# Adjacency tiles as one contiguous piece of a DRAM row, and features read in natural order, in a four-layer graph network

## The chip, the cores and the metric

The kernel runs on one core of a Trainium2 chip. The metric is device time in microseconds (us) of one execution, lower is better. One execution of each kernel is also recorded by the hardware profiler: its span starts with the first instruction and ends with the last. In all that follows the engines are TensorE (PE in the profile, with PEld for its weight loads), VectorE (DVE), ScalarE (ACT), GpSimd (POOL) and SyncE (SP), which here only issues transfers.

## What is computed

There are N = 3327 nodes with D = 64 features and one dense 3327 x 3327 matrix `adj` (with few entries that are not zero). Four layers each normalise the features, apply relu, run a graph network, and add the result to x:

```python
def layer(x, gnn):
    h = jnp.maximum(layernorm(x), 0.0)
    return x + gnn(h, adj)

# gnn 0: two gated cells
m = adj @ (h @ W);  gi = m @ wih.T + bih;  gh = h @ whh.T + bhh
r, z = sigmoid(i_r + h_r), sigmoid(i_z + h_z);  n = tanh(i_n + r * h_n)
h = relu((1 - z) * n + z * h)
# gnn 1: weights by rank of a nonzero in its row, at most the last 100 count
rank = jnp.cumsum(adj != 0, axis=1)
w = mask * jnp.where(pos > 0, 0.5 ** (k - pos), 0.0)
out = w @ (h @ weight) + bias
# gnn 2: three hops with w = adj * adj
x = (w @ x) @ W.T + b
# gnn 3: two hops
x = jnp.tanh(jnp.concatenate([adj @ x, x], axis=1) @ W[k])
```

So the adjacency (or its mask, or its square) is multiplied eight times with 64 features a node: kinds PLAIN, PLAIN, RANKED, SQUARED, SQUARED, SQUARED, PLAIN, PLAIN. In gnn 1 the order of the columns of `adj` matters, since ranks are counted along them; everywhere else a renumbering of the nodes cancels out.

## The kernel before

**Layout.** The 3327 nodes are padded to 3328 = 26 blocks of 128. A node stands at (s, b, p): half s of two, block b of 13 in it, partition p. All work on node features is done for both halves at once: half 0 and half 1 of a chunk share an instruction, the TensorE products for them go to the upper and lower 64 columns of the array side by side. Blocks b are cut into four chunks, `CH[0..3]` = blocks 0-2, 3-5, 6-8, 9-12, so that chunks 0 to 2 have 384 columns per half and chunk 3 has 512. Chunks 0 and 1 form group 0, chunks 2 and 3 group 1. For the last product, chunk 1 is cut in two parts (blocks 3-4 and block 5, `PARTS`).

**Tiles.** The transposed adjacency lies in DRAM as 3328 rows (sources) of 3328 columns (targets). A `Tile(q, g)` is the 128 rows of source block q, and of the columns those of group g, for both halves: two runs of 768 (group 0) or 896 (group 1) fp32 values out of each row, 3,072 or 3,584 bytes each. `load` issues it as one DMA on SP's queue (L411) into one of 20 buffers (`slots`, "adj" in the profile). Each tile serves one or two of the eight products. 234 tiles are loaded in all, 26 for each of nine passes: `alone(0, 0)` is product 0 for group 0, `joint(1, 0)` products 0 and 1 for group 1, `joint(0, 1)` products 1 and 2 for group 0, and so on; `alone(0, 7)` is the last.

**Order.** The order of all instructions is the order in which the program writes them: `run()` walks a list of units (product, chunk, tile) and between them lets small tasks (layernorm, gates, transposes) advance by a budget of estimated microseconds (`spend`). Loads are written ahead while buffers are free. Products are issued at L613. The counts for gnn 1 are made during the first passes: VectorE turns a tile into a 0/1 mask (L472) and TensorE adds the masks up (L548). In product 2, masks are turned into ranks by a product with a triangle (L313 with `tri`), and ScalarE (L529) or VectorE (L527) turn ranks into powers of two. `square` (L446, L448) squares a tile on ScalarE or on VectorE, by the remainder of `q + c` modulo 3.

**Start.** Three DMAs bring the features `xs`: chunk 0 on SP, chunk 1 and then chunks 2 and 3 together on ScalarE's queue (L119), followed there by the weights of the first cell (L153, L156). SP goes on with the tiles. `warm_up` (L176) runs 28 TensorE instructions on the first features. `before_0(c)` computes the layernorm of a chunk on VectorE (L843 to L858), with the power -1/2 on GpSimd (L854). The first product L613 needs this for chunk 0.

**End.** `after_7(c)` evacuates the last product, applies the last dense product (L780) and tanh (L1041), adds to `xs` on VectorE (L1044), and writes the chunk to DRAM by one DMA (L1047): chunks of group 0 on SP, those of group 1 on ScalarE's queue.

**DRAM arrays.** The host lays the features out as [128, 13, 2, 64] (partition, block, half, feature) and takes the output in the same layout, with half s of block b being natural block 13 s + b. The rows and columns of the adjacency are in natural order.

Of the kernel before, what the change touches and what calls it, by code (L numbers as in the profile page):

```python
# [13 lines left out]
ALU = mybir.AluOpType  # L14
# [30 lines left out]
N, D = 3327, 64  # L45
# [38 lines left out]
def chunk_of(b):  # L84
    return next(c for c, (b0, b1) in enumerate(CH[:NC]) if b0 <= b < b1)


def sources_of(*chunks):
    return [s * NB + b for c in chunks for s in range(2) for b in range(*CH[c])]


def upper(n):
    return slice(n * D, (n + 1) * D)
# [3 lines left out]
def kernel(  # L97
# [17 lines left out]


    xs = const.tile([P, NB, 2, D], F32, name="xs")
    for queue, (g0, g1) in ((nc.sync, CH[0]), (nc.scalar, CH[1]), (nc.scalar, (CH[2][0], NB))):
        queue.dma_start(out=xs[:, g0:g1], in_=x[:, g0:g1])  # L119
    slots = [const.tile([P, 2, GWM], F32, name=f"adj{i}") for i in range(NBUF)]  # L120
    mhalf = const.tile([P, 8], F32, name="mhalf")
    nc.gpsimd.memset(mhalf, -0.5)
    bd = const.tile([P, 4, P], F32, name="bd")
# [47 lines left out]
    def warm_up():  # L171

        i, ps = take()
        for n in range(7):
            for h in range(2):
                nc.tensor.matmul(ps[upper(h), :3 * D], xs[:, 0, h, :], xs[:, 0:3, 0], start=True, stop=True)  # L176
        give(i)

    def fold_cell(cell):
# [166 lines left out]
    def groups(t):  # L346
        return t.rearrange("p b s d -> p (b s) d")
# [47 lines left out]
    class Tile:  # L395
# [12 lines left out]
        def load(self):  # L408
            self.slot = dead.popleft()
            w0 = self.b0 * P  # L410
            nc.sync.dma_start(out=slots[self.slot][:, :, :self.w],  # L411
                              in_=adjT[self.q * P:(self.q + 1) * P, :].rearrange(
                                  "p (s w) -> p s w", s=2)[:, :, w0:w0 + self.w])

        def view(self, *c):
            return slots[self.slot][:, :, self.cols(*c) if c else slice(0, self.w)]

        def used(self):
            self.uses -= 1
# [70 lines left out]
    def expand(k, c, t):  # L490

        if k == COUNT:
            return None
        w = width(c)
        if t is SPECIAL:
            g = c // 2
            w0 = (CH[c][0] - CH[GROUPS[g][0]][0]) * P
            finish(NC + 1 + g)
            return lastw[g][:, w0:w0 + w].bitcast(BF16)
        if KIND[k] == PLAIN or (KIND[k] == SQUARED and t.in_place):  # L500
            return t.view(c)
        if KIND[k] == SQUARED:
            room = Mask(t.w)
            wide = room.view.rearrange("p s w -> p (s w)").bitcast(F32)[:, :2 * w].rearrange("p (s w) -> p s w", s=2)
            square(wide, t.view(c), t.q + c)
            squared[k, c, t] = room
            return wide
        wide = work.tile([P, 2, CWM], I16, name="e", bufs=4)[:, :, :w]

        mask_pieces(t=t)
        for s in range(2):
            i, ps = take()
            mm(ps[:, :w], tri, t.mask.view[:, s, t.cols(c)])
            own = chunk_of(t.q % NB) in GROUPS[t.g]
            busy = any((k - 1, ch) in sums for ch in GROUPS[t.g])
            if t.g == 1 and not own and not relief["squares"]:

                on_vector = s and c == GROUPS[1][1]
            elif relief["pieces"]:
                on_vector = s and (t.q + c) % 4
            else:
                on_vector = s and (own if t.g == 0 and (own or busy) else c == GROUPS[t.g][1] or t.g == 1 and not own)
            if on_vector:
                nc.vector.tensor_scalar(wide[:, s], ps[:, :w], BITS, 0.0, op0=ALU.add, op1=ALU.max)  # L527
            else:
# [35 lines left out]
    def last_sources(g):  # L564

        w = sum(width(c) for c in GROUPS[g])
        w0 = CH[GROUPS[g][0]][0] * P
        room = Mask(w)
        v = room.view.rearrange("p s w -> p (s w)").bitcast(F32)
        nc.gpsimd.memset(v, 0.0)  # L570
        yield 4.0
        rows = adjT.rearrange("(q p) (s n) -> q p s n", p=P, s=2)
        for s in range(2):
            nc.sync.dma_start(out=v[s * D:s * D + NQ], in_=rows[:, P - 1, s, w0:w0 + w])
        yield 12.0
        nc.vector.tensor_scalar(v, v, 0.0, 129.0 * TWO7, op0=ALU.not_equal, op1=ALU.mult)
        for c in GROUPS[g]:
            finish(("count", c))
        yield 1.0
        nc.vector.scalar_tensor_tensor(v, totals[g], -TWO7, v, op0=ALU.mult, op1=ALU.add)  # L580
        yield 1.5
        nc.scalar.activation(lastw[g], v, AF.Relu, bias=bitsb)
        room.free()

    def propagate(k, c, t, rhs, first, last):
        if k == COUNT:
            count(t, first, last)
            return
        w = width(c)
        if first:  # L590
            sums[k, c] = [take(sums=True) for _ in range(2 if k == 7 and c == PARTS[1] else 1)]
            sums[k, c] = [sums[k, c][0], sums[k, c][-1]]
        acc = sums[k, c]
        if t is SPECIAL:
            for ch in range(NC):
                while y[k][ch] is None:
                    advance(ch)
            terms = [[lasty[:, h, i, :] for h in range(2)] for i in range(3)]
            rhs = [rhs, rhs]
        else:  # L600
            s, b = divmod(t.q, NB)
            cs = chunk_of(b)
            if y[k][cs] is None:
                finish(cs)
            terms = [[yk[:, b - CH[cs][0], s, :]] * 2 for yk in (y[k][cs] if KIND[k] == RANKED else [y[k][cs]])]
            rhs = [rhs[:, h, :] for h in range(2)]
            if KIND[k] != RANKED:
                t.used()
            if (k, c, t) in squared:
                squared.pop((k, c, t)).free()  # L610
        for n, yq in enumerate(terms):
            for h in range(2):
                nc.tensor.matmul(acc[h][1][h * D:(h + 1) * D, :w], yq[h], rhs[h], start=first and n == 0,  # L613
                                 stop=last and n == len(terms) - 1)
# [102 lines left out]
    def run():  # L717
# [5 lines left out]
        for i, (k, c, t) in enumerate(units):  # L723
# [19 lines left out]
            relief["pieces"] = False  # L743
            if k != 2:
                mask_pieces(1 + len(pieces) // 6)
            elif not (c in GROUPS[0] and (t is SPECIAL or chunk_of(t.q % NB) in GROUPS[0])):
# [88 lines left out]
        for i in {acc[0][0], acc[1][0]}:  # L835
            give(i)

    def layernorm_relu(h, c, scale=None, pace=1.0, squares_on_scalar=False):
        n = 2 * blocks(c)
        v = groups(xchunk(c))  # L840
        st = work.tile([P, 4, 8], F32, name="st", bufs=4)
        xc = work.tile([P, 8, D], F32, name="t2")
        nc.vector.tensor_reduce(st[:, 0, :n], v, AX.X, ALU.add)  # L843
        nc.vector.tensor_scalar(st[:, 1, :n], st[:, 0, :n], 1.0 / D, None, op0=ALU.mult)
        nc.vector.tensor_tensor(xc[:, :n], v, st[:, 1, :n, None].to_broadcast([P, n, D]), ALU.subtract)  # L845
# [87 lines left out]
    def in_three(h, c):  # L933
# [11 lines left out]
        b0, b1 = CH[c]  # L945
        for s in range(2):
            for k in range(2):
                q = k * D + s * NB
# [87 lines left out]
    def after_7(c, acc):  # L1036
# [5 lines left out]
        give(v[0])  # L1042
        yield 0.8
        nc.vector.tensor_tensor(flat(xchunk(c)), flat(xchunk(c)), flat(t), ALU.add)  # L1044
        g0, g1 = CH[c]
        queue = nc.scalar if c in GROUPS[1] else nc.sync
        queue.dma_start(out=out[:, g0:g1], in_=xs[:, g0:g1])  # L1047

    after[:] = [after_0, after_1, after_2, after_3, after_4, after_5, after_6, after_7]

# [66 lines left out]
```

## Time and profile before

| | |
|---|---|
| time, median of 3 runs | 697.6 us (697.42 to 697.65) |
| profiled execution: its own time | 697.73 us |
| profiled execution: span | 695.7 us |
| TensorE granted clock, mean | 0.999 |
| tiles of 768 KB / 896 KB | 130 / 104 |
| read from HBM | 199.45 MB, 288 GB/s over the span |
| DMA packets | 68,693 (7,244 of them under 512 B) |

The page gives each engine's busy time and its share of the span, followed by its number of instructions. Lists of waits give "engine, tile, line <- what it waited for: us in total, times, longest". A line of the timeline has the start in us, the busy time in us, the engine (a "q" behind the name is its queue of issued transfers), the line of the program, the operation, the tiles, and in brackets the idle time of the engine just before, with what ended it.

### The profile page before, as it was taken

To read this page: it belongs to the slowest core of one execution; us is meant where nothing else is said; L and a number is where in the kernel's file an instruction comes from. 1 tells how busy PE (TensorE), PEld (TensorE's weight loads), DVE (VectorE), ACT (ScalarE), POOL (GpSimd) and SP (SyncE) were. 2 spreads that over 40 slices of the span, in tenths; PEclk is the share of its full clock that TensorE was granted. 3 is DMA by queue.
4 is the path that set the end of the run, shared out by engine and by line. 5 is a ranking of instruction groups with operands and counts; after the bars stand their busy time and mean duration, and the time that the engine had idled before them with its cause. 6 is when DMAs were issued, how large, how long until landed. Compare 5 with 4: busy or idle time off the path is not lost.

```text
span 695.7 us, 12589 instructions
## 1 busy us (share of the span) xinstructions
PE 681.0 (98%) x5072; PEld 380.4 (55%) x5072; DVE 355.3 (51%) x772; ACT 274.3 (39%) x426; POOL 77.8 (11%) x114
## 2 busy tenths in 40 slices
PE   7899999999999999999999999999999999999997
PEld 4686667645566785556444444343344444344587
DVE  5946745755997899757341106325271565005101
ACT  1013000403147878888998107722176500000101
POOL 5300000002480414111100000000000000000000
PEclk9999999999999999999999999999999999999999
DMA  9999998099879921792899569954997399917991
GB/s 341 401 400 406 403 407 274 1 349 389 277 242 376 317 96 60 259 316 80 311 361 351 206 216 409 404 227 131 396 370 264 110 399 405 405 75 268 404 403 65
DMA packets 68693, 201.31 MB, mean 289 GB/s; under 512 B 7244, under 2 KB 8372, under 8 KB 68636
## 3 DMA queue, kind: packets, MB, share of 16 engines
q1 hardware_dynamic: 65724, 199.08, 76.9%
q10 hardware_dynamic: 736, 1.23, 0.5%
q8 instruction: 40, 0.66, 0.4%
q0 software_dynamic: 2176, 0.20, 0.2%
q14 instruction: 17, 0.14, 0.0%
HBM read 199.45 MB, written 0.85 MB: 288 GB/s over the span
## 4 chain that ended last, share of the span: by engine, by line
PE 58%; DVE 1%; ACT 0%; POOL 0%; issue 0%; DVEq 0%; ACTq 0%; POOLq 0%
PE sum L613 54%; PE temp L313 3%; PE temp L780 1%; ACT e L529 0%; POOL st L854 0%; DVE both L834 0%; DVE e L527 0%; PE sum L313 0%; ACT both L830 0%; DVE y L858 0%; DVE y L850 0%; DVE t L845 0%; DVE st L851 0%; DVE st L843 0%; DVE xs L865 0%
## 5 line engine op out<-in xcount | busy, mean ns | idle before, releaser
L613 PE MATMUL sum<-adj,y 128*64 128x384 f32 (+3 forms) x3016 | 535.4, 501 | 1.5 <-DVE y L858 0.7
L613 PEld LDWEIGHTS sum<-adj,y 128*64 128x64 f32 x3016 | 248.8, 137 | 230.5 <-issue 196.9
L446 ACT ACTIVATE adj<-adj 128x768 f32<-128x768 f32 (+1 forms) x176 | 144.4, 892 | 45.9 <-PE sum L613 23.0
L472 DVE TENSOR_SCALAR adj<-adj 128x768 bf16<-128x768 f32 (+3 forms) x208 | 114.0, 597 | 32.6 <-PE temp L548 24.7
L613 PE MATMUL sum<-e,both 128*64 128x384 bf16 (+1 forms) x624 | 74.0, 339 | 0.5 <-DVE e L527 0.5
L529 ACT ACTIVATE e<-temp,bitsb 128x384 int16<-128x384 f32 (+1 forms) x120 | 67.8, 607 | 14.9 <-PE temp L313 9.1
L830 ACT COPY both<-sum 64x384 f32<-64x384 f32 (+3 forms) x17 | 8.1, 478 | 148.2 <-PE sum L613 148.2
L834 DVE COPY both<-sum 64x384 f32<-64x384 f32 (+3 forms) x13 | 7.3, 561 | 99.5 <-ACT both L830 98.9
L448 DVE TENSOR_TENSOR adj<-adj 128x768 f32<-128x768 f32 (+1 forms) x32 | 30.6, 1004 | 51.9 <-DMA adj<-in_adjT 33.1
L854 POOL TENSOR_TENSOR st<-st,mhalf 128x6 f32<-128x6 f32 (+1 forms) x16 | 24.9, 1553 | 287.8 <-DVE st L852 287.8
L313 PE MATMUL temp<-adj,tri 128*64 128x384 bf16 (+1 forms) x332 | 51.7, 341 | 1.3 <-ACT e L529 0.8
L613 PEld LDWEIGHTS <-both 128*64 128x64 bf16 x624 | 41.9, 110 | 18.3 <-issue 6.5
L477 POOL DMA_DIRECT2D adj<-totals x52 | 33.6, 648 | 52.6 <-PE temp L313 41.7
L313 PEld LDWEIGHTS <-tri 128*64 128x64 bf16 x416 | 29.2, 110 | 17.3 <-issue 9.8
L527 DVE TENSOR_SCALAR e<-temp 128x384 int16<-128x384 f32 (+1 forms) x46 | 28.3, 615 | 20.0 <-PE temp L313 9.6
L809 DVE STREAM_TRANSPOSE both<-y 32x96 f32<-32x96 f32 (+1 forms) x128 | 35.6, 278 | 2.9
L548 PE MATMUL temp<-adj,behind 128*64 128x384 bf16 x208 | 33.8, 340 | 2.8 <-DVE adj L472 2.6
L825 DVE STREAM_TRANSPOSE y<-t 32x96 f32<-32x96 f32 (+1 forms) x64 | 17.8, 278 | 24.7 <-ACT t L816 23.9
L548 PEld LDWEIGHTS <-behind 128*64 128x64 bf16 x208 | 20.8, 110 | 17.4 <-issue 13.5
L761 DVE COPY t<-sum 128x384 f32<-128x384 f32 x6 | 3.3, 555 | 35.7 <-PE sum L613 35.7
L186 ACT COPY t<-temp 128x128 f32<-128x128 f32 x1 | 0.3, 266 | 48.2 <-PE temp L184 48.2
L570 POOL MEMSET adj<- 128x768 f32 (+1 forms) x2 | 1.6, 800 | 133.2 <-PE sum L613 133.2
(132 smaller groups left out, 353.8 us busy)
## 6 DMA issues: line engine op xcount, KB each, us to landing
adj<-in_adjT SPq DMA_DIRECT2D x130, 768.0 KB, 9.0
adj<-in_adjT SPq DMA_DIRECT2D x104, 896.0 KB, 12.0
xs<-in_x ACTq DMA_DIRECT2D x1, 448.0 KB
adj<-totals POOLq DMA_DIRECT2D x26, 3.0 KB, 4.9
adj<-totals POOLq DMA_DIRECT2D x26, 3.5 KB, 2.3
out<-xs ACTq DMA_DIRECT2D x1, 256.0 KB
xs<-in_x SPq DMA_DIRECT2D x1, 192.0 KB
xs<-in_x ACTq DMA_DIRECT2D x1, 192.0 KB, 3.3
```

What stands on the lines that cost most here:

```text
L313: nc.tensor.matmul(out[hs], lhsT[:, hs], rhs, start=start, stop=stop)
L446: nc.scalar.activation(sq, v, AF.Square)
L448: nc.vector.tensor_tensor(sq, v, v, ALU.mult)
L472: nc.vector.tensor_scalar(t.mask.view[:rows, half], t.view()[:rows, half], 0.0, None, op0=ALU.not_equal)
L477: nc.gpsimd.dma_start(out=t.mask.view[P - 1:P], in_=totals[t.g][t.q:t.q + D + 1:D, :])
L527: nc.vector.tensor_scalar(wide[:, s], ps[:, :w], BITS, 0.0, op0=ALU.add, op1=ALU.max)
L529: nc.scalar.activation(wide[:, s], ps[:, :w], AF.Relu, bias=bitsb)
L548: nc.tensor.matmul(counts[c][1][s * D:(s + 1) * D, :w], behind[:, NQ - 1 - t.q:NQ - 1 - t.q + D], t.mask.view[:, s, t.cols(c)], start=firs ...
L613: nc.tensor.matmul(acc[h][1][h * D:(h + 1) * D, :w], yq[h], rhs[h], start=first and n == 0, stop=last and n == len(terms) - 1)
L809: nc.vector.transpose(to[at:at + 32, :, q], h[q * 32:(q + 1) * 32, :, s, f * 32:(f + 1) * 32])
L825: nc.vector.transpose(yk[q * 32:(q + 1) * 32, :, s, f * 32:(f + 1) * 32], v[at:at + 32, :, q])
L854: nc.gpsimd.tensor_tensor(st[:, 3, :n], st[:, 2, :n], mhalf[:, :n], ALU.pow)
```

## The change

The host side stays as it is: the DRAM arrays keep their natural order. What changes is which natural block stands at position (s, b) in the kernel. `block(s, b)` gives it: for group 0 the six blocks of half 0 are natural blocks 0-5 and those of half 1 blocks 6-11; for group 1 they are blocks 12-18 and 19-25. The columns of a tile, both halves of a group, are then one run in each DRAM row, of 6,144 or 7,168 bytes; in its buffer the two halves follow each other without a gap. `place(q)` is the inverse, used where a tile's source block is looked up among the features.

The features in natural order land in the area of the last tile buffer (`xn`), by four DMAs: blocks 0-2 and 6-8 of both natural halves on SP, 3-5 and 9-12 on ScalarE's queue. `copy_x(c)` copies them into the new positions of `xs` on ScalarE, nine copies in all (`spans` cuts them where natural halves change), written behind the DMAs of the first cell's weights. The first layernorm of chunk 0 reads `xn` itself, and so does the warm-up. The output is written per half and span, by more DMAs, with the second half of the last part on ScalarE's queue. The layernorm's VectorE operations get a view with one more dimension; their sizes are the same.

```diff
 def sources_of(*chunks):
-    return [s * NB + b for c in chunks for s in range(2) for b in range(*CH[c])]
+    return [block(s, b) for c in chunks for s in range(2) for b in range(*CH[c])]
+
+def block(s, b):
+    b0, b1 = (CH[g[i]][i] for g in (GROUPS[b >= CH[2][0]],) for i in (0, 1))
+    return 2 * b0 + s * (b1 - b0) + b - b0
+
+def place(q):
+    return next((s, b) for s in range(2) for b in range(NB) if block(s, b) == q)
+
+def spans(c, s):
+    runs = []
+    for b in range(*CH[c]):
+        sn, bn = divmod(block(s, b), NB)
+        if runs and runs[-1][2] == sn:
+            runs[-1][1], runs[-1][4] = b + 1, bn + 1
+        else:
+            runs.append([b, b + 1, sn, bn, bn + 1])
+    return runs
...
-    for queue, (g0, g1) in ((nc.sync, CH[0]), (nc.scalar, CH[1]), (nc.scalar, (CH[2][0], NB))):
-        queue.dma_start(out=xs[:, g0:g1], in_=x[:, g0:g1])
     slots = [const.tile([P, 2, GWM], F32, name=f"adj{i}") for i in range(NBUF)]
+    xn = slots[NBUF - 1].rearrange("p s w -> p (s w)")[:, :NB * 2 * D].rearrange("p (b s d) -> p b s d", s=2, d=D)
+    for queue, (g0, g1) in ((nc.sync, (0, 3)), (nc.sync, (6, 9)), (nc.scalar, (3, 6)), (nc.scalar, (9, NB))):
+        queue.dma_start(out=xn[:, g0:g1], in_=x[:, g0:g1])
...
-                nc.tensor.matmul(ps[upper(h), :3 * D], xs[:, 0, h, :], xs[:, 0:3, 0], start=True, stop=True)
+                nc.tensor.matmul(ps[upper(h), :3 * D], xn[:, 0, h, :], xn[:, 0:3, 0], start=True, stop=True)
...
-            nc.sync.dma_start(out=slots[self.slot][:, :, :self.w],
-                              in_=adjT[self.q * P:(self.q + 1) * P, :].rearrange(
-                                  "p (s w) -> p s w", s=2)[:, :, w0:w0 + self.w])
+            nc.sync.dma_start(out=slots[self.slot].rearrange("p s w -> p (s w)")[:, :2 * self.w],
+                              in_=adjT[self.q * P:(self.q + 1) * P, 2 * w0:2 * (w0 + self.w)])
...
         def view(self, *c):
-            return slots[self.slot][:, :, self.cols(*c) if c else slice(0, self.w)]
+            both = slots[self.slot].rearrange("p s w -> p (s w)")[:, :2 * self.w].rearrange("p (s w) -> p s w", s=2)
+            return both[:, :, self.cols(*c) if c else slice(0, self.w)]
...
-            own = chunk_of(t.q % NB) in GROUPS[t.g]
+            own = chunk_of(place(t.q)[1]) in GROUPS[t.g]
...
-    def layernorm_relu(h, c, scale=None, pace=1.0, squares_on_scalar=False):
+    def layernorm_relu(h, c, scale=None, pace=1.0, squares_on_scalar=False, source=None):
         n = 2 * blocks(c)
-        v = groups(xchunk(c))
+        v = xchunk(c) if source is None else source
...
+    def copy_x(c):
+
+        for s in range(2):
+            for b0, b1, sn, n0, n1 in spans(c, s):
+                nc.scalar.copy(xs[:, b0:b1, s], xn[:, n0:n1, sn])
+
     def before_0(c):
         h = nodes(c)
-        yield from layernorm_relu(h, c)
+        if c == 0:
+            first = xn[:, 0:2 * CH[2][0], 0].rearrange("p (s b) d -> p b s d", s=2)[:, CH[0][0]:CH[0][1]]
+            yield from layernorm_relu(h, c, source=first)
+        else:
+            yield from layernorm_relu(h, c)
...
-        g0, g1 = CH[c]
-        queue = nc.scalar if c in GROUPS[1] else nc.sync
-        queue.dma_start(out=out[:, g0:g1], in_=xs[:, g0:g1])
+        for s in range(2):
+            queue = nc.scalar if c in GROUPS[1] or s == 1 and c == PARTS[1] else nc.sync
+            for b0, b1, sn, n0, n1 in spans(c, s):
+                queue.dma_start(out=out[:, n0:n1, sn], in_=xs[:, b0:b1, s])
...
     load_cell(0)
+    for c in (1, 0, 2, 3):
+        copy_x(c)
     warm_up()
```

The remaining edits carry the new numbering through: the last rows of all source blocks are read from the new columns, the last sources' features go to the new rows, and the test that decides when masks are made looks the source block up with `place`.

More of the change, by code (lines that the diff above doesn't have):

```diff
@@ L571, in last_sources @@
         yield 4.0
-        rows = adjT.rearrange("(q p) (s n) -> q p s n", p=P, s=2)
+        rows = adjT.rearrange("(q p) n -> q p n", p=P)
         for s in range(2):
-            nc.sync.dma_start(out=v[s * D:s * D + NQ], in_=rows[:, P - 1, s, w0:w0 + w])
+            nc.sync.dma_start(out=v[s * D:s * D + NQ], in_=rows[:, P - 1, 2 * w0 + s * w:2 * w0 + (s + 1) * w])
         yield 12.0
@@ L600, in propagate @@
         else:
-            s, b = divmod(t.q, NB)
+            s, b = place(t.q)
             cs = chunk_of(b)
@@ L745, in run @@
                 mask_pieces(1 + len(pieces) // 6)
-            elif not (c in GROUPS[0] and (t is SPECIAL or chunk_of(t.q % NB) in GROUPS[0])):
+            elif not (c in GROUPS[0] and (t is SPECIAL or chunk_of(place(t.q)[1]) in GROUPS[0])):
                 mask_pieces(1)
@@ L836, in evacuate_stacked @@
             give(i)
-    def layernorm_relu(h, c, scale=None, pace=1.0, squares_on_scalar=False):
+    def layernorm_relu(h, c, scale=None, pace=1.0, squares_on_scalar=False, source=None):
         n = 2 * blocks(c)
-        v = groups(xchunk(c))
+        v = xchunk(c) if source is None else source
         st = work.tile([P, 4, 8], F32, name="st", bufs=4)
         xc = work.tile([P, 8, D], F32, name="t2")
-        nc.vector.tensor_reduce(st[:, 0, :n], v, AX.X, ALU.add)
+        nc.vector.tensor_reduce(st[:, 0, :n].rearrange("p (b s) -> p b s", s=2), v, AX.X, ALU.add)
         nc.vector.tensor_scalar(st[:, 1, :n], st[:, 0, :n], 1.0 / D, None, op0=ALU.mult)
-        nc.vector.tensor_tensor(xc[:, :n], v, st[:, 1, :n, None].to_broadcast([P, n, D]), ALU.subtract)
+        mean = st[:, 1, :n].rearrange("p (b s) -> p b s", s=2)[:, :, :, None].to_broadcast([P, blocks(c), 2, D])
+        nc.vector.tensor_tensor(xc[:, :n].rearrange("p (b s) d -> p b s d", s=2), v, mean, ALU.subtract)
         yield 1.5 * pace
@@ L947, in in_three @@
             for k in range(2):
-                q = k * D + s * NB
+                q = k * D + block(s, b0) - b0
                 nc.gpsimd.dma_start(out=lasty[q + b0:q + b1, k], in_=room[P - 1:P, :, s])
         return terms
+    def copy_x(c):
+        for s in range(2):
+            for b0, b1, sn, n0, n1 in spans(c, s):
+                nc.scalar.copy(xs[:, b0:b1, s], xn[:, n0:n1, sn])
     def before_0(c):
         h = nodes(c)
-        yield from layernorm_relu(h, c)
+        if c == 0:
[3 more added lines that the diff above has]
+            yield from layernorm_relu(h, c)
         y[0][c] = h
```

## The prediction

> **What bounds the kernel now.** I read the page first (engine sums, slices), then the list of what TensorE waited for, then windows, and last the timeline of the two ends.
>
> ```profile
> PE 681.0 (98%) x5072; PEld 380.4 (55%) x5072; DVE 355.3 (51%) x772; ACT 274.3 (39%) x426; POOL 77.8 (11%) x114
> ...
> PE temp L176 <- DMA xs<-in_x: 3.9, 1, 3.9
> PE temp L548 <- DVE adj L472: 2.6, 4, 1.3
> ...
> PE sum L613 <- DMA adj<-in_adjT: 0.4, 2, 0.3
> ```
>
> TensorE is busy for 681.0 of 695.7 us. Of the 14.7 us left, 3.9 lie before its first instruction, 3.6 after its last, and 7.2 in gaps between. In the long stages four L613 instructions of 384 columns take 0.645 us (the chain of waits has 256 in 41.28 us), so busy there is work. For adjacency tiles it waited 0.4 us in all. The transfers are elsewhere:
>
> ```profile
> 20.00:30.00 10.00, 8.49 (x81) 6.64 (x77) 9.77 (x26) 1.21 (x3) 3.49 (x2) 1.00 1.03 401
> 30.00:40.00 10.00, 9.87 (x82) 8.41 (x83) 7.33 (x16) 2.12 (x4) 0.59 (x1) 1.00 1.03 401
> 40.00:50.00 10.00, 10.00 (x75) 8.01 (x73) 4.12 (x8) 1.06 (x2) 0.00 (x0) 1.00 1.03 401
> 120.00:140.00 20.00, 20.00 (x132) 12.78 (x130) 15.06 (x38) 7.62 (x14) 0.00 (x0) 1.00 0.03 5
> ```
>
> Columns: length, then PE, PEld, DVE, ACT and POOL busy, clock, DMA share, GB/s. The DMA engines are full until about 105 us, then fall idle because all buffers hold tiles: the stream is ahead. Between 20 and 30 us VectorE, at 9.77 of 10, sets the pace.
>
> ```profile
> 0.81 0.39 SPq L119 DMA_DIRECT2D xs<-in_x  x1
> 3.90 0.55 DVE L843 TENSOR_REDUCE st<-xs 128x6 f32<-128x384 f32 x1 [3.90 <-DMA xs<-in_x]
> 4.61 1.28 ACT L799 ACT_TABLE_LOAD   x1 [4.61 <-DMA xs<-in_x]
> 8.09 0.56 DVE L858 SCALAR_TENSOR_TENSOR y<-t,st 128x384 f32<-128x384 f32 x1 [0.21 <-POOL st L854]
> 8.71 2.80 PE L613 MATMUL sum<-adj,y 128*64 128x384 f32 x16 [0.18 <-DVE y L858]
> 13.64 0.87 PE L613 MATMUL sum<-adj,y 128*64 128x384 f32 x4 [0.19 <-DMA adj<-in_adjT]
> 18.70 0.48 PE L548 MATMUL temp<-adj,behind 128*64 128x384 bf16 x3 [0.78 <-DVE adj L472]
> 21.81 0.49 PE L548 MATMUL temp<-adj,behind 128*64 128x384 bf16 x3 [1.30 <-DVE adj L472]
> 58.12 0.87 PE L613 MATMUL sum<-adj,y 128*64 128x384 f32 x4 [0.26 <-DMA adj<-in_adjT]
> ```
>
> Features land at 3.90, the layernorm of chunk 0 takes 4.75 us, and the first adjacency product starts at 8.71. The end is serial too:
>
> ```profile
> 692.30 0.63 DVE L1044 TENSOR_TENSOR xs<-xs,t 128x256 f32<-128x256 f32 x2 [0.59 <-ACT t L1041]
> 690.35 3.24 SPq L1047 DMA_DIRECT2D out<-xs  x3
> L1047 SPq DMA_DIRECT2D out<-xs x3: 367/378/392, 690.4 to 693.2; - x3
> L292 SPq DMA_DIRECT2D w<-in_weights x4: 598/609/615, 114.6 to 117.2; - x4
> ```
>
> The last two lines give shortest, median and longest issue in ns: one run per partition about 0.38 us, two runs of 256 B 0.61.
>
> **What the Trainium skill says.** "DMA: Bandwidth & Descriptors", section "Why small descriptors are slow (HBM only)", gives each packet a fixed cost of about three cycles, so fewer and longer pieces should move the same bytes faster. The trace agrees: its packets of 1,536, 3,072 and 3,584 B took 65, 121 and 140 ns (medians), a line of 27.3 B/ns plus about 9 ns. I use this line. "TensorE: Matmul & The Clock Gate", section "What's actually happening", says a window of about 3.4 us without work brings TensorE back to half clock. The granted clock rises at 8.26 us, during the warm-up products (L176), and falls at 694.3, after the last product. The gap below is 1.2 us; I assume it is too short.
>
> **Tiles in one piece.** 16 packets of 3,072 B per engine and tile (16 x 121 = 1.94 us, the observed spacing) become 8 of 6,144 B: by the line 8 x 234 = 1.87. Gain 0.064 us a tile, 1.7 us by tile 25, if such a piece stays one packet. TensorE would use it only where it waits for tiles: 0.19 us at 13.6, 0.26 at 58.1. Everything between waits for VectorE or for TensorE itself. Tile 25 lands at 58.07 and would land at 56.4, so the 0.26 goes. After that no wait for a tile reaches TensorE. Issue by SP falls from 0.54 to about 0.4 us a tile, hidden: SP waits for buffers.
>
> **Features.** Chunk 0 now needs two loads on SP (192 KB each). The first lands near 3.9, and the warm-up still starts there. The second moves beside ScalarE's 256 KB; the old third load landed at 5.12, after the same 832 KB, so I take 4.9 (bounds 4.6 and 5.2). SP's first tile is issued one load later, but waits behind the same bytes: nothing. The nine copies queue on ScalarE behind four DMA issues and the table load, from about 5.9; priced by its copies (0.27 us at 128 elements, 0.47 at 384) they sum to 2.8 us, done near 8.8, and ScalarE's next work was at 12.2. Chunk 1's two copies are ready near 6.6; VectorE wants them at 7.5. Should that cover fail, chunk 1 slips but has 2 us before its transposes. Chunk 0 skips the copies. The feature area is the last buffer, loaded again only some 20 us later: no wait.
>
> So the layernorm chain and the first product move by 1.0 us. Tiles 1 to 3 are waiting by then, so TensorE catches up 0.4 by 15 us. But GpSimd's chain (power, then memsets to 19.7) moves by the full 1.0; VectorE waits for it at 19.76 (L272), and from there to 30 us VectorE is full and TensorE waits for its masks. Hence 1.0 us late at 30 us, less the 0.26 at 58: **+0.74 us** (0.2 to 1.2).
>
> **Output.** The last chunks are written per half. SP issues chunk 4 in two parts of two runs (0.6 us each) where one took 0.37, and only then the half of chunk 5; its other half goes on ScalarE, behind nothing. Last issue start: 692.75 + 2 x 0.67 (with the gaps seen) = 694.09 instead of 693.21, +0.88; the smaller transfer gives back 0.1: **+0.8 us** (0.4 to 1.2). Chunk 0's two issues (from 690.35, 1.3 us) fit before. The group 1 outputs, near 651 and 660 us, are hidden under products.
>
> **Order of work.** TensorE has the same products in the same order. The new numbers shift which squares and which expansions (L529, L527) fall to VectorE: one 384-column expansion in all moves to ScalarE, 0.6 us. Between 200 and 335 us TensorE's gaps sum to some 3 us, so this is worth 0 with bounds -0.7 and +0.7. Numbering, spans and the count row cost no instruction.
>
> Sum: 0.74 + 0.8 + 0 = 1.5 us. The profiled execution took 697.73 (span 695.7 and 2.0 around it), so 699.3; the median of the runs is 0.1 lower: **699.1 us**.
>
> **Rivals.**
> 1. Start and end slip as said: 699.1. Chance 0.58. Own range 698.3 to 700.0.
> 2. The stream paces the start: TensorE follows the landings up to about tile 30, so the faster stream buys 30 x 0.066 = 2.0 us, the later start is swallowed, and only the output costs: 697.6 - 2.0 + 0.8 = 696.4. For it: DMA full at 401 GB/s, and both tile waits. Against: the larger waits name VectorE. It decides if the first tiles' masks are no longer what TensorE waits for near 20 us. Chance 0.14.
> 3. The work order between 200 and 335 us or a start quickly caught up takes the losses back: near 698.2. For: those gaps are sensitive to a fraction of a microsecond; against: they are short already. Chance 0.16.
> 4. The gap between warm-up and first product halves the clock for one window: 3.4 us at half speed, 1.7 us of work lost, on top of mine: 700.8. It decides if the window beginning at 8.26 counts as idle; it would be two thirds busy. Chance 0.12.
> That long pieces are cut into packets as before would cost the gain of 1.7 us, which I don't count on: within case 1.
>
> **Range and chances.** 0.2% of 697.6 is 1.4 us, about what this measurement can tell from no change. My forecast lies only just beyond it. Case 1 falls about two to one on the slower side (0.41 and 0.17), case 4 wholly (0.12), case 3 on no change (0.16), case 2 is split: 0.06 faster, 0.08 no change, since its losses may also stay away. Slower 0.53, same 0.41, faster 0.06. Range 697.1 to 700.9: it leaves out most of case 2 and a little at the top.
>
> **What would show it.** The packet count falls from 68,693 to about 41,500 (half of the 59,904 tile packets go, some 2,700 output packets come) and the first windows show 410 to 415 GB/s; the first layernorm reduce starts near 4.9, the first L613 near 9.7, and the masks still hold TensorE near 20 us; the wait at 58 is gone; the last output issue is near 1.5 us later than before, by the clock of the span. Wrong if the first product starts before 9.2, if TensorE runs ahead of its former times at 60 us, or if the stretch from 200 to 335 us changes by over 1 us.

## The result and the profile after

The changed kernel takes 699.16 us (median of 14 executions, 698.8 to 699.51); the kernel before, on the same chip in the same session, 697.64 (14 executions, 697.42 to 697.87). The ratio is 1.0021, 95% interval 1.0014 to 1.0029: 1.5 us slower. The profiled execution took 699.23, its span 697.0.

Two lines of the page of the changed kernel, engine sums and packets:

```profile
PE 681.4 (98%) x5072; PEld 381.9 (55%) x5072; DVE 353.5 (51%) x771; ACT 277.0 (40%) x436; POOL 77.8 (11%) x114
...
DMA packets 41670, 201.32 MB, mean 289 GB/s; under 512 B 10684, under 2 KB 11428, under 8 KB 41612
```

The same products, 0.4 us more of busy TensorE, and 27,000 packets fewer for the same bytes. So the tiles do arrive in longer pieces. TensorE's idle time is 15.6 us of the span instead of 14.7, which makes 0.9 of the 1.3 us that the span is longer. What it waited for, from the changed kernel's list of waits (us in total, times, longest):

```profile
PE temp L197 <- DMA adj<-in_x: 3.9, 1, 3.9
PE sum L634 <- DVE y L880: 2.7, 2, 2.2
PE temp L569 <- DVE adj L493: 1.6, 4, 0.7
```

(L634, L569, L493 and L880 were L613, L548, L472 and L858.) The waits for tiles are gone, and the waits for masks fell from 2.6 to 1.6 us. In their place stands one of 2.2 us for chunk 0's layernorm (L880). The windows show the faster stream (columns as in the prediction):

```profile
10.00:20.00 10.00, 10.00 (x72) 5.13 (x74) 6.02 (x13) 1.89 (x4) 8.32 (x18) 0.83 1.02 420
20.00:30.00 10.00, 9.00 (x85) 7.12 (x83) 9.79 (x25) 1.21 (x3) 2.31 (x4) 1.00 1.01 415
30.00:40.00 10.00, 9.66 (x81) 7.83 (x78) 8.45 (x21) 1.94 (x4) 1.97 (x1) 1.00 1.01 414
40.00:50.00 10.00, 10.00 (x75) 8.10 (x73) 3.31 (x7) 1.24 (x3) 0.00 (x0) 1.00 1.02 419
```

414 to 420 GB/s where 401 stood. Between 20 and 30 us VectorE is as full as before, 9.79 of 10. In the first row the clock is 0.83, which the kernel before did not have. The timeline of the start:

```profile
0.81 0.87 SPq L141 DMA_DIRECT2D adj<-in_x  x2
...
3.90 3.80 PE L197 MATMUL temp<-adj 128*64 128x192 f32 x28 [3.90 <-DMA adj<-in_x]
...
5.07 0.55 DVE L864 TENSOR_REDUCE st<-adj 128x6 f32<-128x384 f32 x1 [5.07 <-DMA adj<-in_x]
...
5.71 2.32 ACT L978 COPY xs<-adj 128x192 f32<-128x192 f32 x9
...
9.88 4.50 PE L634 MATMUL sum<-adj,y 128*64 128x384 f32 x16 [2.18 <-DVE y L880]
...
18.08 0.72 DVE L187 COPY cells<-temp 64x192 f32<-64x192 f32 x2 [2.39 <-POOL both L272]
...
20.67 0.48 PE L569 MATMUL temp<-adj,behind 128*64 128x384 bf16 x3 [0.29 <-DVE adj L493]
...
23.19 0.49 PE L569 MATMUL temp<-adj,behind 128*64 128x384 bf16 x3 [0.71 <-DVE adj L493]
```

The layernorm's first operation starts at 5.07 instead of 3.90, the first product at 9.88 instead of 8.71: both 1.17 us later. The masks of the last row come at 23.19 instead of 21.81, 1.38 later. The first 16 products take 4.50 us instead of 2.80, at half clock. The timeline of the end:

```profile
691.14 3.81 SPq L1080 DMA_DIRECT2D out<-xs  x5
...
692.67 0.60 ACT L1073 ACTIVATE t<-temp 128x256 f32<-128x256 f32 x2 [0.38 <-PE temp L801]
693.09 0.63 DVE L1076 TENSOR_TENSOR xs<-xs,t 128x256 f32<-128x256 f32 x2 [0.58 <-ACT t L1073]
693.75 0.35 ACTq L1080 DMA_DIRECT2D out<-xs  x1
```

The last additions to `xs` start 0.79 us later than before (693.09 against 692.30). TensorE ends at 692.90, 0.80 later, and from there to the end of the span there are 4.12 us instead of 3.60. The loss in the span, 1.3 us, is the sum of these two.

### The profile page after: what moved, and what is told of

Its sections match the earlier page's. It is cut to its first block, busy times and chain, and to the rows that moved or that the text cites. A ratio compares the mean times of both kernels' runs of the same rounds, so it can differ in the third digit from the quotient of the medians.

```text
span 697.0 us, 12626 instructions
## 1 busy us (share of the span) xinstructions
PE 681.4 (98%) x5072; PEld 381.9 (55%) x5072; DVE 353.5 (51%) x771; ACT 277.0 (40%) x436; POOL 77.8 (11%) x114
## 2 busy tenths in 40 slices
DMA packets 41670, 201.32 MB, mean 289 GB/s; under 512 B 10684, under 2 KB 11428, under 8 KB 41612
## 4 chain that ended last, share of the span: by engine, by line
PE 58%; DVE 1%; ACT 0%; POOL 0%; issue 0%; DVEq 0%; ACTq 0%; POOLq 0%
PE sum L634 54%; PE temp L334 3%; PE temp L801 1%; ACT e L550 0%; POOL st L876 0%; DVE both L855 0%; DVE e L548 0%; PE sum L334 0%; ACT both L851 0%; DVE y L872 0%; DVE y L880 0%; DVE t L867 0%; DVE st L873 0%; DVE st L864 0%; DVE xs L887 0%
## 5 line engine op out<-in xcount | busy, mean ns | idle before, releaser
L634 PE MATMUL sum<-adj,y 128*64 128x384 f32 (+3 forms) x3016 | 537.1, 502 | 3.1 <-DVE y L880 2.7
L634 PEld LDWEIGHTS sum<-adj,y 128*64 128x64 f32 x3016 | 250.3, 137 | 231.9 <-issue 190.0
L493 DVE TENSOR_SCALAR adj<-adj 128x768 bf16<-128x768 f32 (+3 forms) x208 | 113.6, 595 | 32.6 <-PE temp L569 24.7
L634 PE MATMUL sum<-e,both 128*64 128x384 bf16 (+1 forms) x624 | 74.0, 339 | 0.5 <-DVE e L548 0.4
L469 DVE TENSOR_TENSOR adj<-adj 128x768 f32<-128x768 f32 (+1 forms) x32 | 30.6, 1003 | 46.5 <-DMA adj<-in_adjT 27.3
L634 PEld LDWEIGHTS <-both 128*64 128x64 bf16 x624 | 42.0, 110 | 18.1 <-issue 6.5
L548 DVE TENSOR_SCALAR e<-temp 128x384 int16<-128x384 f32 (+1 forms) x47 | 28.8, 614 | 21.1 <-PE temp L334 10.5
L569 PE MATMUL temp<-adj,behind 128*64 128x384 bf16 x208 | 33.9, 340 | 1.7 <-DVE adj L493 1.6
L569 PEld LDWEIGHTS <-behind 128*64 128x64 bf16 x208 | 21.0, 110 | 16.0 <-issue 12.1
L550 ACT ACTIVATE e<-sum,bitsb 128x384 int16<-128x384 f32 (+1 forms) x27 | 15.9, 589 | 3.1 <-PE sum L334 1.6
```

Source lines behind the costliest of these rows:

```text
L469: nc.vector.tensor_tensor(sq, v, v, ALU.mult)
L493: nc.vector.tensor_scalar(t.mask.view[:rows, half], t.view()[:rows, half], 0.0, None, op0=ALU.not_equal)
L569: nc.tensor.matmul(counts[c][1][s * D:(s + 1) * D, :w], behind[:, NQ - 1 - t.q:NQ - 1 - t.q + D], t.mask.view[:, s, t.cols(c)], start=firs ...
```

## The experiments

Each kernel was compared with the kernel before in its own session, where that had 697.68 to 697.70 us. The first four cut the change into its parts.

**The tiles alone.** Numbering, contiguous tiles and buffers as in the change; the host lays features and output out in the new order and puts the output back, so that start and end are those of the kernel before.

```diff
+    order = np.array([[block(s, b) for s in range(2)] for b in range(NB)])
...
-        "in_x": np.ascontiguousarray(xp.reshape(2, NB, P, D).transpose(2, 1, 0, 3)),
+        "in_x": np.ascontiguousarray(xp.reshape(NQ, P, D)[order].transpose(2, 0, 1, 3)),
...
-    return np.ascontiguousarray(got.transpose(2, 1, 0, 3).reshape(NP, D)[:N])
+    full = np.empty((NQ, P, D), got.dtype)
+    full[order] = got.transpose(1, 2, 0, 3)
+    return np.ascontiguousarray(full.reshape(NP, D)[:N])
```

> Contiguous tiles and the new numbering alone: the host lays features and output out in the new order, so start and end are written as before. My steps (start +0.74, of which -0.26 is the tile wait at 58 us; output +0.8; order of work 0) give 697.6 - 0.3 = 697.3, with 697.0 to 697.7; the first L634-type product near 8.7 us, tile 25 landed near 56.4, masks still the wait near 20 us. Rival 'the stream paces the start': 695.6 (2.0 us gained). Rival 'the order of work between 200 and 335 us matters': off 697.3 by more than 0.5 with the difference lying in that stretch.

Measured: 696.98 us (13 executions, 696.73 to 697.29), ratio 0.999 [0.9982, 0.9998]. Faster by 0.7 us, more than the 0.26 of the prediction's sum. Its timeline where the tile wait of 0.26 us had been, and then that of the changed kernel:

```profile
57.24 0.62 PE L568 MATMUL temp<-adj,behind 128*64 128x384 bf16 x4
...
57.57 0.94 PE L633 MATMUL sum<-adj,y 128*64 128x384 f32 x4
```

```profile
58.62 0.62 PE L569 MATMUL temp<-adj,behind 128*64 128x384 bf16 x4
...
58.95 0.94 PE L634 MATMUL sum<-adj,y 128*64 128x384 f32 x4
```

There is no wait left. With the tiles alone the product starts 0.33 us after the mask products that stand before it (they start at 57.24, as in the kernel before), and at 57.57 instead of 58.12: 0.55 us earlier. In the changed kernel the same product comes at 58.95, late by the new start. The list of waits had shown only 0.26, because it counts idle time from the end of the mask products (0.62 us after their start), while the next product can start before they end. TensorE ends at 691.55, also 0.55 earlier than before.

**Tiles and the new start.** The features in natural order, with their loads, copies and layernorm source, on top of the tiles; output as before, in the host's order.

```diff
-    for queue, (g0, g1) in ((nc.sync, CH[0]), (nc.scalar, CH[1]), (nc.scalar, (CH[2][0], NB))):
+    for queue, (g0, g1) in ((nc.sync, (0, 3)), (nc.sync, (6, 9)), (nc.scalar, (3, 6)), (nc.scalar, (9, NB))):
...
+    for c in (1, 0, 2, 3):
+        copy_x(c)
```

> Contiguous tiles with the changed kernel's start (four loads, copies on ScalarE), output written as before with the host putting it in order. By the trace of the changed kernel TensorE ends 0.8 us later than before: 698.4 (698.1 to 698.7), so 1.1 over the tiles alone. If the start is swallowed (rival 'the stream paces the start'), within 0.2 of the tiles alone.

Measured: 699.44 us (7, 699.12 to 700.41), ratio 1.0026 [1.0015, 1.0037]; 1.0 more than expected. TensorE ends at 692.68, 1.13 later than with the tiles alone, about as expected. The rest lies behind TensorE's end: 4.41 us instead of 3.58, with the same code there. The run on the odd tail (below) takes this apart.

**Tiles and the new output.** The old start, the output by halves.

```diff
-        queue = nc.scalar if c in GROUPS[1] else nc.sync
-        queue.dma_start(out=out[:, g0:g1], in_=xs[:, g0:g1])
+        for s in range(2):
+            queue = nc.scalar if c in GROUPS[1] or s == 1 and c == PARTS[1] else nc.sync
+            for b0, b1, sn, n0, n1 in spans(c, s):
+                queue.dma_start(out=out[:, n0:n1, sn], in_=xs[:, b0:b1, s])
```

> Contiguous tiles with the start as before (features laid out by the host) and the changed kernel's output (per half, more issues on SP). By the trace of the changed kernel the last issue is 0.5 us later against TensorE's end: 0.5 over the tiles alone, 697.8 (697.5 to 698.1). If the output cost what I predicted, 0.8 over the tiles alone. If the rest of the 1.5 us came from the middle, equal to the tiles alone.

Measured: 697.53 us (13, 697.36 to 697.99), ratio 0.9999 [0.9991, 1.0007]: 0.55 above the tiles alone. The output costs 0.55 us.

**The order of the feature loads.** The whole change, but the second load that chunk 0 needs goes first on ScalarE's queue.

```diff
-    for queue, (g0, g1) in ((nc.sync, (0, 3)), (nc.sync, (6, 9)), (nc.scalar, (3, 6)), (nc.scalar, (9, NB))):
+    for queue, (g0, g1) in ((nc.sync, (0, 3)), (nc.scalar, (6, 9)), (nc.sync, (3, 6)), (nc.scalar, (9, NB))):
```

> The changed kernel with chunk 0's two feature loads first on two queues (blocks 0-2 on SP, 6-8 on ScalarE's) and the others second. If the start costs because chunk 0's second load is SP's second, the first layernorm reduce moves from 5.07 back to about 4.1, the first product from 9.88 to about 8.9, and the time falls by 0.8 to 1.0: 698.3. If the start costs because of the copies on ScalarE, the time stays at 699.2 or grows, as chunk 1's loads now come second.

Measured: 698.03 us (13, 697.6 to 698.97), ratio 1.0004 [0.9996, 1.0012]: 1.13 less than the changed kernel, from one line. A line of its timeline:

```profile
4.30 0.56 DVE L864 TENSOR_REDUCE st<-adj 128x6 f32<-128x384 f32 x1 [4.30 <-DMA adj<-in_x]
```

The layernorm starts at 4.30 instead of 5.07. This profiled execution is the slowest of the thirteen (698.97 us): its first tile landed late, and the first product began only at 9.63. With the same loads in the run with both edits (below) it began at 8.97, and TensorE ended at 691.85, 1.05 earlier than in the changed kernel. Against the kernel with the tiles and the output alone (697.53) the start is left with 0.5 us, and the layernorm is 0.4 later than in it.

**More of the output on ScalarE.** The second half of the larger part (chunk 4) on ScalarE's queue too, to shorten SP's row of three issues.

```diff
-            queue = nc.scalar if c in GROUPS[1] or s == 1 and c == PARTS[1] else nc.sync
+            queue = nc.scalar if c in GROUPS[1] or s == 1 and c in PARTS else nc.sync
```

> The changed kernel with the second half of chunk 4's output on ScalarE's queue too, so that SP has two issues at the end instead of three. If the last issue on SP sets the end (in the changed kernel's trace it starts at 694.52, after two issues of 0.37 and 0.46 us), it starts near 694.0 and the time falls by 0.5: 698.7. If the landing of the small pieces sets it, the time stays at 699.2.

Measured: 699.68 us (9, 699.2 to 700.16), ratio 1.0026 [1.0017, 1.0036]. The expectation failed, by its sign. The end of this kernel's timeline:

```profile
692.42 0.38 ACT L1073 ACTIVATE t<-temp 128x256 f32<-128x256 f32 x1 [0.38 <-PE temp L801]
692.84 0.43 DVE L1076 TENSOR_TENSOR xs<-xs,t 128x256 f32<-128x256 f32 x1 [0.58 <-ACT t L1073]
693.30 0.47 ACTq L1080 DMA_DIRECT2D out<-xs  x1
693.87 0.28 ACT L1073 ACTIVATE t<-temp 128x128 f32<-128x128 f32 x1 [1.06 <-DVE xs L1076]
694.18 0.29 DVE L1076 TENSOR_TENSOR xs<-xs,t 128x128 f32<-128x128 f32 x1 [0.91 <-ACT t L1073]
694.50 0.37 ACTq L1080 DMA_DIRECT2D out<-xs  x1
```

ScalarE waits with the issue at 693.30 for VectorE's addition, and the tanh of the last part, written behind it, starts only at 693.87; in the changed kernel the two tanh stand in one row from 692.67. The last issue starts at 694.50 again, although TensorE ended 0.25 us earlier in this execution (692.65). From TensorE's end to the end of the span there are 4.57 us instead of 4.12, which is most of the loss.

**A longer warm-up.** The changed kernel with `range(11)` for `range(7)` in `warm_up`, so that TensorE is not idle before its first product.

```diff
-        for n in range(7):
+        for n in range(11):
```

> The changed kernel with 11 instead of 7 rounds of warm-up products, which fill most of the gap before the first product (2.2 us in the changed kernel's trace). If the fallen clock costs something, no execution has a mean granted clock below 0.998 and the median is 699.0, against 699.16 with the executions at 0.997 near 699.35. If the lost half window is covered by the wait for masks near 20 us, no difference: 699.2. If the longer warm-up itself delays the first product, 699.4 or more.

Measured: 699.02 us (16, 698.71 to 699.46), ratio 1.0019 [1.0011, 1.0026]: 0.14 below the changed kernel, which was timed in another session; not to be told apart. No execution had a clock below 0.999. Its timeline:

```profile
3.92 6.44 PE L197 MATMUL temp<-adj 128*64 128x192 f32 x44 [3.92 <-DMA adj<-in_x]
...
10.19 2.75 PE L634 MATMUL sum<-adj,y 128*64 128x384 f32 x16
```

The 16 products run at full clock, but start at 10.19, because the warm-up now stands in their way.

**Both edits together,** the order of loads and the half of chunk 4 on ScalarE.

```diff
-    for queue, (g0, g1) in ((nc.sync, (0, 3)), (nc.sync, (6, 9)), (nc.scalar, (3, 6)), (nc.scalar, (9, NB))):
+    for queue, (g0, g1) in ((nc.sync, (0, 3)), (nc.scalar, (6, 9)), (nc.sync, (3, 6)), (nc.scalar, (9, NB))):
...
-            queue = nc.scalar if c in GROUPS[1] or s == 1 and c == PARTS[1] else nc.sync
+            queue = nc.scalar if c in GROUPS[1] or s == 1 and c in PARTS else nc.sync
```

> The changed kernel with chunk 0's loads first on two queues and the second half of chunk 4's output on ScalarE's queue. First loads alone gave 698.03; half a microsecond less at the end gives 697.5 (697.2 to 697.8), level with before. If the two don't add up (end set by landing), 698.0.

Measured: 698.46 us (21, 698.06 to 699.04), ratio 1.0011 [1.0004, 1.0017]: 0.43 worse than the order of loads alone. The second edit loses here what it lost before.

**The odd tail.** In the kernel with tiles and the new start, the last output's semaphore is the first of eight that SP looks at before it ends; the landing is followed by seven more looks of some 0.06 us. Here an earlier load is cut into eight, so that the last output gets the last of the eight.

```diff
-        nc.sync.dma_start(
-            out=brow[:, 0:3],
-            in_=bass.AP(tensor=bias_rows.tensor, offset=bias_rows.offset, ap=[[0, P], [D, 3], [1, D]]),
-        )
+        for p in range(0, P, P // 8):
+            nc.sync.dma_start(
+                out=brow[p:p + P // 8, 0:3],
+                in_=bass.AP(tensor=bias_rows.tensor, offset=bias_rows.offset, ap=[[0, P // 8], [D, 3], [1, D]]),
+            )
```

> The kernel with contiguous tiles and the changed start, old output, with one bias load near 140 us cut into 8 loads of 16 partitions, whose issue is hidden. It turns the round of semaphores by 7, so that the last output uses the last of the eight that SP looks at when the program ends, as before the change, instead of the first. If that order cost 0.4 us in the run without it (699.44, SP's seven further looks of 0.06 us after the last landing), 699.0; if the slow last landing of that run came from the semaphore's place too, 698.4; if neither, 699.4.

Measured: 699.07 us (15, 698.39 to 699.41), ratio 1.0018 [1.001, 1.0026]: 0.37 less. The order of the looks is worth that much, and the kernel with 699.44 overstated the start by it. The other 0.3 to 0.4 of the tail stays (3.85 us behind TensorE's end here, 4.41 before, 3.58 with the tiles alone): in the two traces the last output lands 1.98 and 1.85 us after its issue, instead of 1.59 with the tiles alone. In both an instruction fetch of 8,192 bytes occupies a DMA engine at that time (0.67 us from 694.12 in the first, 0.55 us from 694.41 in the second); that it is the cause was not tried. In the profiled executions of the other kernels at most two looks follow the last landing, so there this order is worth 0.12 us at most.

**Long pieces or numbering?** The tiles alone, with two runs per row in the buffer, which leaves the gap of 896 columns as before.

```diff
-            nc.sync.dma_start(out=slots[self.slot].rearrange("p s w -> p (s w)")[:, :2 * self.w],
-                              in_=adjT[self.q * P:(self.q + 1) * P, 2 * w0:2 * (w0 + self.w)])
+            nc.sync.dma_start(out=slots[self.slot][:, :, :self.w],
+                              in_=adjT[self.q * P:(self.q + 1) * P, 2 * w0:2 * (w0 + self.w)].rearrange(
+                                  "p (s w) -> p s w", s=2))
```

> The tiles alone, with the new numbering and the same DRAM runs, but with the buffers laid out as before, 896 columns from half to half, so that a row has two destinations. If the 0.7 us that the tiles alone gained come from longer packets, the packets are 3,072 B again and the time goes back to 697.6 (gap before tile 25 at 57.6 to 58.1 back). If they come from the new numbering, 697.0.

Measured: 697.55 us (13, 697.39 to 697.73), ratio 0.9998 [0.999, 1.0006]. The packet lines of the pages of the tiles alone and of this kernel:

```profile
DMA packets 38741, 201.31 MB, mean 290 GB/s; under 512 B 7244, under 2 KB 8372, under 8 KB 38684
```

```profile
DMA packets 55381, 201.31 MB, mean 289 GB/s; under 512 B 7244, under 2 KB 8372, under 8 KB 55324
```

The difference is 130 tiles x 128 packets: the tiles of group 0 come in two packets a row again (those of group 1 fill their buffer without a gap and stay whole). And the wait is back, in this kernel's timeline:

```profile
57.33 0.62 PE L568 MATMUL temp<-adj,behind 128*64 128x384 bf16 x4
...
58.12 0.87 PE L633 MATMUL sum<-adj,y 128*64 128x384 f32 x4 [0.16 <-DMA adj<-in_adjT]
```

At 58.12, as before the change. So the 0.6 us that separates the two kernels belongs to the long packets of group 0, and the numbering is worth nothing that can be measured.

**The last part on ScalarE.** The tiles alone, with the smaller last part (chunk 5) on ScalarE's queue, where no computation is behind it.

```diff
-        queue = nc.scalar if c in GROUPS[1] else nc.sync
+        queue = nc.scalar if c in GROUPS[1] or c == PARTS[1] else nc.sync
```

> The tiles alone, with the last part's output (64 KB) issued on ScalarE's queue, where nothing is behind it, instead of on SP behind the issue of the part before. The last issue starts 0.4 us earlier: 696.6 (696.4 to 696.8). If the landing of the larger part before it sets the end, 696.9.

Measured: 696.90 us (21, 696.74 to 697.26), ratio 0.9989 [0.9982, 0.9995]. It is the lowest of all, but within 0.1 of the tiles alone: the number of the second expectation, though not its reason. The larger part's 128 KB, issued at 691.90, are seen as landed at 693.65, and the smaller part behind them at 693.84, so the last issue still sets the end. It starts only 0.2 us earlier against TensorE's end (0.86 us behind it, 692.11 less 691.25, instead of 1.08), since ScalarE has to wait for VectorE's addition, and its transfer takes 1.72 us to land instead of 1.59.

**Both halves of the last part on ScalarE,** with the better order of loads.

```diff
-            queue = nc.scalar if c in GROUPS[1] or s == 1 and c == PARTS[1] else nc.sync
+            queue = nc.scalar if c in GROUPS[1] or c == PARTS[1] else nc.sync
```

> Chunk 0's loads first on two queues, and both halves of the last part on ScalarE's queue, where nothing is behind them; SP has chunk 4's two halves. The last issues then start near 0.4 us (ScalarE) and 0.5 us (SP) earlier than with the changed kernel's queues: 698.03 - 0.4 = 697.6. In the version with chunk 4's second half on ScalarE, the tanh of the last part waited behind that issue; if this was not the reason for its loss, 698.0 or more.

Measured: 697.91 us (13, 697.33 to 698.32), ratio 1.0002 [0.9994, 1.0011]: 0.55 better than with chunk 4's half on ScalarE. That fits the tanh behind the issue as the cause of the loss there, though two pieces changed queues between these two kernels. The forecast of 697.6 was missed: against the order of loads alone it wins only 0.12, less than the spread of either. The last four pieces are issued between 692.52 and 693.12, and the last of them is seen as landed at 694.91, 1.79 us after its issue; in the changed kernel that took 1.55 (694.52 to 696.07).

## Why the prediction was right, and where its terms were not

The forecast of 699.1 us stands beside 699.16, and its mechanism, a later start and a later end against little use of faster tiles, is what the runs show. That the number fits within 0.1 us is luck in part: its terms are off by up to 0.6 us and cancel. Taken from the medians of the kernels:

| step | forecast, us | measured, us | from |
|---|---|---|---|
| tiles | -0.26 | -0.7 | tiles alone less before |
| start | +1.0 | +1.6 | the changed kernel less tiles and output |
| output | +0.8 | +0.55 | tiles and output less tiles alone |
| order of work, 200 to 335 us | 0 | -0.1 | the same product is 0.88 us later than before at 200 us, 0.80 at 335; contained in the steps above |
| sum | +1.54 | +1.5 | |

The kernel before, the tiles alone, tiles and output, and the changed kernel form a chain, so the measured steps add up by construction; only the single steps test the prediction.

**Tiles.** The line of 27.3 B/ns plus 9 ns holds: packets of 6,144 B took 234 ns, as forecast, and those of 7,168 B 272. Tile 25 landed at 56.41 (forecast 56.4), and 41,670 packets stand against 41,500. The term that failed is "so the 0.26 goes": 0.55 went, by the timeline at 58 us. The 0.26 had been read off a wait that is counted from the modelled end of pipelined products. The median gained another 0.16. Executions differ by that and more: in two further kernels with the old start and the new tiles (tiles and output; the last part on ScalarE) TensorE ended at 691.25, 0.85 earlier than before. Of the Trainium skill's rule ("DMA: Bandwidth & Descriptors", section "Why small descriptors are slow (HBM only)") the direction held here even above 3 KB: merging two pieces of 3,072 B into one took 3% off.

**Start.** The bound of the second load (4.6 to 5.2) held with 5.07, the forecast's 4.9 was 0.17 too early. The copies took 2.32 us from 5.71, hidden as forecast (2.8 from 5.9). Rival 4, given 0.12, took place in the profiled execution, at a smaller price. In windows of the changed kernel:

```profile
6.59:10.00 3.41, 1.23 (x16) 0.79 (x14) 3.06 (x8) 1.44 (x6) 1.34 (x1) 1.00 1.03 380
10.00:13.41 3.41, 3.41 (x12) 1.32 (x14) 1.90 (x5) 0.00 (x0) 2.25 (x3) 0.50 1.02 420
13.41:16.82 3.41, 3.41 (x32) 1.83 (x30) 2.28 (x3) 0.95 (x2) 3.22 (x6) 1.00 1.01 416
```

The clock rose at 6.59 in this execution, not at 8.26; the warm-up thus ran faster and ended at 7.70, and the gap to the first product was 2.18 us, not 1.2. In the next window the clock is 0.50. I had priced that at 1.7 us on top of all. It cost far less, because TensorE then waits for VectorE's masks in any case: those waits near 20 us fell from 0.78 and 1.30 to 0.29 and 0.71. The four executions with a mean clock of 0.997 took 699.35 us on average, the other ten, at 0.999 or 1.000, 699.04. TensorE's end says the same: 1.35 later than with the tiles alone here, 1.43 in the odd tail's kernel, whose clock fell too; 1.13 in the kernel with tiles and start and 1.10 in the one with more of the output on ScalarE, whose clocks stayed at 1.00. So the clock's share is 0.2 to 0.3 us where it falls.

The shift by 1.0 was meant to travel through GpSimd to VectorE's operation on `bcol` (L272 of the kernel before). Where the clock stayed up, it did. The same operation with the tiles alone, and then with tiles and start:

```profile
19.75 0.28 DVE L292 TENSOR_SCALAR t<-t,bcol 64x128 f32<-64x128 f32 x1 [0.41 <-POOL t L287]
```

```profile
20.90 0.28 DVE L293 TENSOR_SCALAR t<-t,bcol 64x128 f32<-64x128 f32 x1 [0.41 <-POOL t L288]
```

It comes 1.15 us later, after the same wait for GpSimd, and TensorE's products are 1.14 us later from there on, until the tiles give their share back at 58 us. In the two kernels in which TensorE ended at 691.25 this wait for GpSimd happened to end at 19.43 and 19.46, 0.3 earlier, and the 0.3 lasts to the end. So GpSimd carries the shift, as far as traces show it; no run changed its chain alone. In the profiled execution of the changed kernel the half clock took its place: the operation starts at 21.14 without a wait. Before it VectorE had waited 2.39 us at L187, for a TensorE product (L184) that ended at 17.97 as well as for GpSimd's memset (L272 of the changed kernel, another line than the prediction's), which ended at 18.05.

That the load order causes the start's cost is shown: one line gives back 1.13. Of this the layernorm's earlier start is 0.8 to 0.9 (4.30 and, with both edits, 4.16 instead of 5.07). The rest fits the clock: with this order no execution had a mean below 0.998, where four of fourteen had 0.997, and the gap before the first product was 1.02 us with both edits, instead of 2.18. The two shares were not measured apart.

Net of the tile wait, TensorE ends 0.80 us late; forecast 0.74. In the changed kernel's trace the same product is 1.38 us late at 30 us (forecast 1.0), and the tiles give back 0.55 at 58 us (forecast 0.26). Both terms were too small, by about the same amount.

**Output.** The number of issues and their order were right; their price was not, and so neither was the last one's delay. The row of output issues on SP in the changed kernel (shortest, median, longest in ns):

```profile
L1080 SPq DMA_DIRECT2D out<-xs x5: 373/434/564, 691.1 to 694.5; - x5
```

0.43 us against the 0.61 that I had taken from loads of weights into 64 partitions. The last issue started 1.31 us later by the clock of the span, 0.80 of it TensorE's and 0.51 its own, where the forecast had 0.88.

**Rivals 2 and 3.** Rival 2 (the stream paces the start, 696.4) is out: without the new start and output, the whole faster stream is worth 0.7 us, not 2.0, and masks still hold TensorE near 20 us (waits of 0.71 and 1.31 with the tiles alone). Rival 3 is out: between 200 and 335 us only 0.08 us came back (0.88 to 0.80).

**Open.** The changed kernel's time is 2.2 us above its span, the kernel before's 2.0. These 0.2 us are in the medians, and no view shows them.

## What to carry to other kernels

A transfer that becomes faster is worth only the waits for it, so look for those first, and read their size from when the next product could have been issued, not from the idle time that the list shows. When data is rearranged for one long stream, look at what the rearrangement does to the first load and the last store: here one extra load ahead of the first layernorm cost more than the whole stream gained. Before a store is moved to a compute engine's queue, see what that engine has behind it.

## What the runs showed of the hardware that was not expected

- A window of TensorE's clock need not be empty to halve the next: 1.23 us of work in 3.41 and a gap of 2.18 us sufficed. Windows of the odd tail's kernel and then of the kernel with tiles and start:

```profile
6.84:10.25 3.41, 1.40 (x16) 0.80 (x14) 3.06 (x8) 1.31 (x6) 1.34 (x1) 1.00 1.03 369
```

```profile
7.40:10.81 3.41, 1.71 (x16) 0.83 (x14) 3.06 (x8) 0.71 (x3) 1.34 (x1) 1.00 1.02 377
```

The first, with 1.40 us of work, was followed by half clock; the second, with 1.71, was not. So in these traces the line lies between the two. The Trainium skill ("TensorE: Matmul & The Clock Gate", section "What's actually happening") speaks of an idle window of about 3.4 us; here the measurement decides. The windows do not start with the work: the clock rose at 6.59, at 8.26 and at 9.34 us in different executions, with the first warm-up products at 3.90 to 3.92.
- Which of the eight semaphores the last output uses changed the time by 0.37 us (699.44 to 699.07).
- One of the sixteen parts of a transfer can slip at the start. In the profiled execution of the better load order, fifteen parts of tile 0 had landed at 7.30 us and the last at 9.50 (all at 7.28 in the changed kernel). Its clock rose only at 13.53, and its first 16 products took 4.71 us instead of 2.80; its mean clock of 0.999 does not count the time before the rise. That execution took 698.97 with a median of 698.03.
